# Four layers in one kernel: layer 1's taps from a queue, gate products on another engine, group norms' products in other places, the first input in thirds

## The chip, the cores and the metric

One core of a Trainium2 chip. The kernel's engines run side by side and meet at semaphores: TensorE (PE, with its weight loads PEld), VectorE (DVE), ScalarE (ACT), GpSimd (POOL) and SyncE (SP, which issues most DMAs). The metric is the device time of one execution, in microseconds. Every engine works through its own list of instructions in order; where an instruction waits, everything behind it on that engine waits too.

## What is computed

The input x is four images of 256 channels and 48 x 48 positions, in float32. Four layers follow, each `x = x + layer(group_norm(x))`:

- Layer 0: attention over the 2,304 positions with 8 heads of 64 and normed queries and keys, then a projection.
- Layer 1: a gate. The normed x goes through a 3x3 maximum and a blur with stride 3 to a 16 x 16 map; four depthwise convolutions with long, thin kernels are summed; a sigmoid of that, enlarged to 48 x 48, multiplies the normed x.
- Layer 2: one attention of width 64 over all positions, a projection, and a batch norm over the four images.
- Layer 3: a channel gate, a 3x3 depthwise convolution, an instance norm and a leaky ReLU.

```python
s = x_h1 + x_w1 + x_h2 + x_w2                  # four depthwise convolutions of the 16 x 16 map
gate = jax.nn.sigmoid(att)                     # att: s after a batch norm with given statistics
gate_up = gate[:, :, idx_h][:, :, :, idx_w]
return x[:, :c] * gate_up
...
x = x + _L1_conv_ref(_gn(x), ...)              # _gn: 32 groups of 8 channels
```

## The kernel before

Channels lie on the partitions, in two halves (k = 0, 1) of 128. Three images' x stay in SBUF; the fourth takes the first one's place when that has been sent to DRAM.

**Order.** The order of instructions on all five engines is written out by hand (`manual_schedule`): each engine's list is the order in which the Python code emits. `attend` (L393) walks over a list of *groups*. A group is two blocks of 128 keys against 384 queries of a pair of heads. Nine groups (slots 0 to 8) make a *unit*, six units a *phase* (one pair of heads of one image), four phases an image. So there are 16 phases of layer 0, 864 groups; then four phases of three units for layer 2, and after them layer 3.

For group t, `attend` emits: the score matmuls (L246) and the exponentials on ACT (L252); then the sum of the previous group's exponentials (`add_up`: L277 on POOL adds two of them into `half`, L286 and L292 on DVE add into `acc`); what is `due`; in slot 2 one early step of the layer-1 lane; the `fills` of this slot, sorted by a rank; the other lanes; and last the value matmuls (L266) of the previous group, after a unit's end also the copy of their sums on ACT (L339).

**Slot 2 (AT_AFTER % 9)** holds the chunk of the next pair's projection. By rank: 1, q's matmuls and its eviction on ACT (L528, L544); 2, v's (L559, L564); 2.5, the first half of the output projection of an earlier unit (L610 on PE, L615 on DVE, which adds the result to x); 3, k's matmuls, its eviction and two sums of squares on ACT (L550); 4, the second half of the output projection. (For image 0 the first half has rank 0.) Jobs without a rank count as 5. All of these take PSUM tiles from one pool of two, `pj`, so a matmul waits until an earlier tile has been read by ACT or DVE.

**Layer 1** of images 0 to 2 runs as a lane in the layer-0 phases of the next image (`l1_all`), that of image 3 in layer 2's phases, in another form (`l1_last`). A lane is a generator; `paced` lets it take its steps in chosen slots. Its parts: a group norm `gn`, `maxima` (DVE, L727 to L763, also ahead of the fills of slot 2), `padded`, then `strips`: 81 taps, each a product of a shifted 16 x 16 window with a per-channel weight on ACT (L789). They go in 20 rounds, five taps in the first and four in the others, two rounds ahead of the round that DVE adds up (L807), through three buffers. A round is a step, taken in slots 2, 4, 6 and 8. Then `gated`: the sigmoid by an exponential, and for three thirds of x a product with the gate (L913, on POOL for images 0 to 2, on DVE for image 3) and an addition on DVE (L915).

**`gn`** gathers statistics (L182), joins them (L187), and needs two small matmuls with `gmat` to spread them over a group's channels (L190, L200), each with some small DVE work, the second with a power on POOL (L165); the results are `rs`, `nm` and `nb`. It is a lane as well, so its matmuls stand at the end of whichever slot its steps fall into.

**Start.** `load_x(0)` brings image 0's halves, one DMA from SP and one from ACT; DVE takes statistics of 12 pieces (L179), `gn` follows, then the weights are scaled on ACT (L491), and the first projections run (L528). ACT also issues the small constants' loads (L113 to L134) and loads its function table (L154).

Of the kernel before, what the change touches and what calls it, by code (L numbers as in the profile page):

```python
# [9 lines left out]
F32 = mybir.dt.float32  # L10
# [4 lines left out]
P = 128  # L15
# [59 lines left out]
def usual_path(  # L75
# [28 lines left out]
    def load_x(b):  # L104
        for k in range(NK):
            eng = nc.scalar if b == 0 and k else nc.sync
            eng.dma_start(X[b][:, k, :], xv[:, k, b, :])

# [61 lines left out]

    def gn(b, res, halves=range(NK), slices=range(NSL), first=False):

        if "st" not in res:
            res["st"] = small.tile([P, NK, NSL, 6], F32, tag="gn_st", name="gn_st")
        st = res["st"]
        if first:
            for k in halves:
                for s in slices:
# [10 lines left out]
        ps = pj_tile()  # L189
        nc.tensor.matmul(ps[:, 0:NK], lhsT=gmat, rhs=mv[:, :, 0], start=True, stop=True)  # L190
        gm = small.tile([P, NK], F32, tag="gn_gm", name="gn_gm")
        nc.vector.tensor_copy(gm, ps[:, 0:NK])
        dev = small.tile([P, NK], F32, tag="gn_dev", name="gn_dev")
        nc.vector.tensor_sub(dev, mv[:, :, 0], gm)
        sq = small.tile([P, NK], F32, tag="gn_sq", name="gn_sq")
        nc.vector.tensor_mul(sq, dev, dev)
        nc.vector.tensor_add(sq, sq, mv[:, :, 1])
        yield 2
        ps = pj_tile()
        nc.tensor.matmul(ps[:, 0:NK], lhsT=gmat, rhs=sq, start=True, stop=True)  # L200
        gv = small.tile([P, NK], F32, tag="gn_gv", name="gn_gv")
        nc.vector.tensor_scalar(gv, ps[:, 0:NK], GN_EPS, None, ALU.add)
        rs = small.tile([P, NK], F32, tag="gn_rs", name="gn_rs", bufs=6)
        rsqrt(rs, gv)
        yield 2
        nm = small.tile([P, NK], F32, tag="gn_nm", name="gn_nm", bufs=6)
        nc.vector.tensor_scalar(nm, gm, -1.0, None, ALU.mult)
        nb = small.tile([P, NK], F32, tag="gn_nb", name="gn_nb", bufs=6)
        nc.vector.tensor_mul(nb, nm, rs)
        res["rs"], res["nb"], res["nm"] = rs, nb, nm  # L210
        yield 1
# [156 lines left out]
    due, fills, clock = {}, {}, {}  # L368

    FREE = 10**6  # L370
    AT_TOTAL, AT_FOLD, AT_INVERT, AT_DIVIDE, AT_AFTER = 3, 2, 5, 9, 11

# [20 lines left out]
    def attend(phases):  # L393
# [22 lines left out]
        def do(table, t, which=lambda rank: True):  # L416

            jobs = [job if isinstance(job, tuple) else (5, job) for job in table.pop(t, ())]
            table[t] = [job for job in jobs if not which(job[0])]
            for _, fn in sorted((job for job in jobs if which(job[0])), key=lambda job: job[0]):  # L420
                fn()

        for t, (u, g, st) in enumerate(groups):
# [18 lines left out]
            if prev is not None:  # L442
# [3 lines left out]
                if pg == NG - 1:  # L446
                    last(pu, t)
            prev = (u, g)
        pu, pg = prev
# [327 lines left out]
    def strips(b, k, norm, res):  # L777
# [6 lines left out]
        ]  # L784

        def products(n):
            for i, t in enumerate(ROUNDS[n]):
                dr, dc = TAPS[t]
                nc.scalar.activation(  # L789
                    bufs[n % 3][:, :, min(n, 1) + i].rearrange("p (r c) -> p r c", c=AS),  # L790
                    pd[:, PAD + dr : PAD + dr + AS, PAD + dc : PAD + dc + AS],
                    AF.Identity, scale=wt[:, k, t : t + 1],
                )

# [95 lines left out]
    def gated(b, k, norm, res):  # L890
# [19 lines left out]
        for i in range(4):  # L910
            if i < 3:
                eng = nc.gpsimd if b < NX else nc.vector
                eng.tensor_mul(xg[:, :, i], xg[:, :, i], up)  # L913
            if i > 0:
# [142 lines left out]
    def l1_all(b):  # L1057
# [3 lines left out]
        start = clock["t"]  # L1061
        ahead = gn(b, norm)
        for _ in range(NSL - 1):
# [10 lines left out]
        for k in range(NK):  # L1074
# [109 lines left out]
    for i, (b, p) in enumerate(order):  # L1184
# [1296 lines left out]
```

## Time and profile before

| | us |
|---|---|
| time, median of 3 runs (range) | 3,684.39 (3,683.62 to 3,686.41) |
| the profiled execution | 3,686.69 |
| its span, first to last instruction | 3,685.0 |
| first score matmul of layer 0's groups | 47.5 |
| first score matmul of layer 2's groups | 2,965.1 |

Rows of the page's costliest groups (line, engine, operation, output and inputs, count, then busy time and the mean of one in ns, then the engine's idle time before them and what ended it):

```profile
L252 ACT ACTIVATE pt<-sc 128x768 f32<-128x768 f32 x1944 | 1476.4, 812 | 790.0 <-PE sc L246 787.5
L277 POOL TENSOR_TENSOR half<-pt 128x768 f32<-128x768 f32 x477 | 939.9, 1972 | 1729.0 <-ACT pt L252 1650.1
L292 DVE TENSOR_TENSOR acc<-acc,pt 128x768 f32<-128x768 f32 x792 | 885.2, 1118 | 84.4 <-DVE acc L292 2.3
L789 ACT ACTIVATE prod<-pd,wt 128x256 f32<-128x256 f32 x486 | 280.9, 745 | 0.2
```

Durations of one instruction overlap the next one's where an engine is busy without a break, so the distance from start to start is the better price there; both are told where they differ. An idle time before a matmul with a name behind it is a wait; what is idle on another engine costs nothing by itself.

### The profile page before, as it was taken

To read this page: it belongs to the slowest core of one execution; us is meant where nothing else is said; L and a number is where in the kernel's file an instruction comes from. 1 tells how busy PE (TensorE), PEld (TensorE's weight loads), DVE (VectorE), ACT (ScalarE), POOL (GpSimd) and SP (SyncE) were. 2 spreads that over 40 slices of the span, in tenths; PEclk is the share of its full clock that TensorE was granted. 3 is DMA by queue.
4 is the path that set the end of the run, shared out by engine and by line. 5 is a ranking of instruction groups with operands and counts; after the bars stand their busy time and mean duration, and the time that the engine had idled before them with its cause. 6 is when DMAs were issued, how large, how long until landed. Compare 5 with 4: busy or idle time off the path is not lost.

```text
span 3685.0 us, 86525 instructions
## 1 busy us (share of the span) xinstructions
PE 3516.1 (95%) x36338; PEld 1766.9 (48%) x36338; DVE 2520.1 (68%) x3209; ACT 2343.6 (64%) x3814; POOL 1423.6 (39%) x899
## 2 busy tenths in 40 slices
PE   8999999999999999999999999999999999999685
PEld 4554545554444444544444445444444445654343
DVE  3455555476778676767786667667967787576687
ACT  4565666566875885568758856687587555555353
POOL 2333333333343334333433343334333456664232
PEclk9999999999999999999999999999999999999797
DMA  2111111111111111311111111111111100000001
GB/s 90 47 26 22 26 21 25 21 29 18 26 21 25 21 25 21 76 21 25 21 25 21 25 21 25 21 25 21 25 17 25 17 6 6 6 8 4 26 34 70
DMA packets 112959, 95.53 MB, mean 26 GB/s; under 512 B 56128, under 2 KB 110000, under 8 KB 110768
## 3 DMA queue, kind: packets, MB, share of 16 engines
q1 hardware_dynamic: 109952, 87.73, 13.0%
q8 instruction: 286, 4.69, 0.5%
q10 hardware_dynamic: 2608, 2.18, 0.2%
q14 instruction: 113, 0.93, 0.1%
HBM read 56.97 MB, written 11.80 MB: 19 GB/s over the span
## 4 chain that ended last, share of the span: by engine, by line
PE 71%; DVE 14%; issue 6%; ACT 5%; POOL 4%; DMA 1%; SPq 0%; DVEq 0%; ACTq 0%; POOLq 0%
PE sc L246 27%; PE av L266 27%; PE pj L528 6%; DVE acc L292 5%; PE pj L610 3%; PE pj L559 3%; POOL half L277 2%; DVE sc L1471 2%; ACT pt L252 2%; PE pj L299 1%; ACT prod L789 1%; DVE av L1471 1%; PE pj L851 1%; DVE acc L286 1%; PE pj L967 1%
## 5 line engine op out<-in xcount | busy, mean ns | idle before, releaser
L252 ACT ACTIVATE pt<-sc 128x768 f32<-128x768 f32 x1944 | 1476.4, 812 | 790.0 <-PE sc L246 787.5
L277 POOL TENSOR_TENSOR half<-pt 128x768 f32<-128x768 f32 x477 | 939.9, 1972 | 1729.0 <-ACT pt L252 1650.1
L246 PE MATMUL sc<-q,k 64*64 64x384 f32 x13824 | 1280.1, 485 | 9.8 <-ACT pt L252 9.4
L266 PE MATMUL av<-pt,v 64*64 64x384 f32 x13824 | 1280.4, 485 | 0.0
L292 DVE TENSOR_TENSOR acc<-acc,pt 128x768 f32<-128x768 f32 x792 | 885.2, 1118 | 84.4 <-DVE acc L292 2.3
L246 PEld LDWEIGHTS sc<-q,k 64*64 64x64 f32 x13824 | 510.1, 133 | 636.2 <-issue 498.7
L266 PEld LDWEIGHTS av<-pt,v 64*64 64x64 f32 x13824 | 514.7, 133 | 590.7 <-issue 554.8
L292 DVE TENSOR_TENSOR acc<-acc,half 128x768 f32<-128x768 f32 x459 | 473.6, 1032 | 349.2 <-POOL half L277 348.3
L615 DVE SCALAR_TENSOR_TENSOR x<-pj,bo,x 128x384 f32<-128x384 f32 x192 | 118.2, 616 | 512.3 <-PE pj L610 512.0
L789 ACT ACTIVATE prod<-pd,wt 128x256 f32<-128x256 f32 x486 | 280.9, 745 | 0.2
L528 PE MATMUL pj<-xs,w 128*128 128x384 f32 (+1 forms) x720 | 275.4, 505 | 0.0
L347 POOL TENSOR_TENSOR o<-o,rinv 128x384 f32<-128x384 f32 x95 | 125.9, 1326 | 238.7 <-DMA rinv<-rinv 224.5
L528 PEld LDWEIGHTS pj<-xs,w 128*128 128x128 f32 x720 | 124.1, 189 | 127.9 <-issue 38.3
L610 PE MATMUL pj<-o,wo 128*128 128x384 f32 x384 | 160.7, 503 | 22.1 <-DVE x L615 17.9
L266 PE MATMUL av<-pt,qv 64*64 64x384 f32 x1728 | 174.6, 497 | 0.0
L246 PE MATMUL sc<-qv,kd 64*64 64x384 f32 x1728 | 169.7, 486 | 2.4 <-ACT pt L252 2.4
L807 DVE TENSOR_REDUCE prod<-prod 128x256 f32<-128x1280 f32 x114 | 168.6, 1479 | 0.0
L559 PEld LDWEIGHTS pj<-w,xs 128*128 128x128 f32 x1080 | 134.5, 191 | 24.1
L286 DVE TENSOR_TENSOR acc<-pt 128x768 f32<-128x768 f32 x99 | 131.7, 1331 | 12.5 <-ACT pt L252 12.5
L559 PE MATMUL pj<-w,xs 128*128 128x128 f32 x1080 | 134.9, 275 | 0.0
L544 ACT ACTIVATE k<-pj,bias 128x384 f32<-128x384 f32 x90 | 52.2, 580 | 106.6 <-PE pj L528 106.2
L343 POOL TENSOR_TENSOR o<-raw 128x384 f32<-128x384 f32 x95 | 112.2, 1182 | 0.0
(235 smaller groups left out, 2716.6 us busy)
## 6 DMA issues: line engine op xcount, KB each, us to landing
xs<-in_x_dram SPq DMA_DIRECT2D x90, 384.0 KB
rinv<-rinv SPq DMA_DIRECT2D x208, 94.5 KB
out_dram<-x SPq DMA_DIRECT2D x6, 1152.0 KB
l<-row SPq DMA_DIRECT2D x416, 1.5 KB
w<-in_wqkv_dram SPq DMA_DIRECT2D x32, 192.0 KB
x<-in_x_dram SPq DMA_DIRECT2D x5, 1152.0 KB
rinv<-ls SPq DMA_DIRECT2D x208, 1.5 KB
x_out<-x SPq DMA_DIRECT2D x6, 384.0 KB
```

The costliest lines, as they stand in the source:

```text
L246: nc.tensor.matmul(ps[c * D : (c + 1) * D, h, :SL], lhsT=u["of"]["k"][r, j0 : j0 + D], rhs=u["of"]["q"][r, u["qc"]], start=True, stop=True,)
L252: nc.scalar.activation(pt, ps[:, :, :SL], AF.Exp, scale=u["scale"])
L266: nc.tensor.matmul(u["av"][h * D : (h + 1) * D, half, :SL], lhsT=value(u, j, h)[r], rhs=pt[r, h, :], start=j == 0, stop=j == JB - 1,)
L277: nc.gpsimd.tensor_add(half, pts[0], pts[1])
L286: nc.vector.tensor_add(u["acc"], ready[0], ready[1])
L292: nc.vector.tensor_add(u["acc"], u["acc"], term)
L347: eng.tensor_mul(o, o, u["rinv"])
L528: nc.tensor.matmul(ps[:, :n], lhsT=at["w"][:, k, t, :], rhs=xs[s][:, k, :n], start=k == 0, stop=k == NK - 1,)
L559: nc.tensor.matmul(ps[:, i * P : (i + 1) * P], lhsT=xs[s][:, k, i * P : (i + 1) * P], rhs=at["w"][:, k, 2, :], start=k == 0, stop=k == NK - 1,
L610: nc.tensor.matmul(ps[:, :SL], lhsT=wo[:, p, k * P : (k + 1) * P], rhs=o["o"], start=True, stop=True,)
L789: nc.scalar.activation(bufs[n % 3][:, :, min(n, 1) + i].rearrange("p (r c) -> p r c", c=AS), pd[:, PAD + dr : PAD + dr + AS, PAD + dc : PA ...
L807: nc.vector.tensor_reduce(to, bufs[n % 3][:, :, : min(n, 1) + len(taps)], AX.X, ALU.add)
```

## The change

- `load_x(0)` issues each half in three parts of 768 columns, half by half in turn; the statistics of image 0 are taken in the order of the columns.
- `gn` has its two matmuls and what follows them in functions, and a way to place them: with `placed=True` the first goes, as a fill of rank 3.5, into the next slot 2, the second into slot 2 of the unit after, and `nb` is worked out three slots later. It is used for both norms of `l1_all` and for the next image's layer-0 norm; `l1_all` waits for `nb` before its taps.
- `strips` puts taps into a queue, `taps_due`. After a fill of rank 1, 2, 3 or 4 one is taken; at the end of a slot as many as `QUOTA` names; before a round is added up, whatever is left of it.
- The gate's products of images 0 to 2 run on DVE.

```diff
     def load_x(b):
-        for k in range(NK):
-            eng = nc.scalar if b == 0 and k else nc.sync
-            eng.dma_start(X[b][:, k, :], xv[:, k, b, :])
+        parts = 3 if b == 0 else 1
+        for i in range(parts):
+            cols = slice(i * N // parts, (i + 1) * N // parts)
+            for k in range(NK):
+                eng = nc.scalar if b == 0 and k else nc.sync
+                eng.dma_start(X[b][:, k, cols], xv[:, k, b, cols])
...
-    def gn(b, res, halves=range(NK), slices=range(NSL), first=False):
+    def gn(b, res, halves=range(NK), slices=range(NSL), first=False, placed=False):
...
+        def squares():
+            ps = pj_tile()
+            nc.tensor.matmul(ps[:, 0:NK], lhsT=gmat, rhs=mv[:, :, 0], start=True, stop=True)
+            nc.vector.tensor_copy(gm, ps[:, 0:NK])
...
+        def inverse():
+            ps = pj_tile()
+            nc.tensor.matmul(ps[:, 0:NK], lhsT=gmat, rhs=res["sq"], start=True, stop=True)
...
+        if placed:
+            t = clock["t"] + 1
+            t += (AT_AFTER - t) % NG
+            fills.setdefault(t, []).append((3.5, squares))
+            fills.setdefault(t + NG, []).append((3.5, inverse))
+            due.setdefault(t + NG + 3, []).append(done)
+            yield 1
+            return
...
+    taps_due = []
+    QUOTA = (2, 1, 0, 1, 2, 1, 2, 1, 2)
+    def take_taps(n):
+        for _, fn in taps_due[:n]:
+            fn()
+        del taps_due[:n]
+    EVICTED = (1, 2, 3, 4)
...
-            for _, fn in sorted((job for job in jobs if which(job[0])), key=lambda job: job[0]):
+            for rank, fn in sorted((job for job in jobs if which(job[0])), key=lambda job: job[0]):
                 fn()
+                if rank in EVICTED:
+                    take_taps(1)
...
                 if pg == NG - 1:
                     last(pu, t)
+            take_taps(QUOTA[clock["slot"]])
...
         def products(n):
             for i, t in enumerate(ROUNDS[n]):
-                dr, dc = TAPS[t]
-                nc.scalar.activation(
...
+                taps_due.append((n, lambda i=i, t=t: tap(n, i, t)))
...
         for n, taps in enumerate(ROUNDS):
             last = n == len(ROUNDS) - 1
+            take_taps(sum(1 for of, _ in taps_due if of <= n))
...
-                eng = nc.gpsimd if b < NX else nc.vector
-                eng.tensor_mul(xg[:, :, i], xg[:, :, i], up)
+                nc.vector.tensor_mul(xg[:, :, i], xg[:, :, i], up)
...
-        ahead = gn(b, norm)
+        ahead = gn(b, norm, placed=True)
...
+            while "nb" not in norm:
+                yield ROUND
             yield from strips(b, k, norm, res)
...
-        yield from gn(b, norm2, [1])
+        yield from gn(b, norm2, [1], placed=True)
...
-            others.append((gn(b + 1, norms0[b + 1]), GN_TICKS, 0, n - 2))
+            others.append((gn(b + 1, norms0[b + 1], placed=True), NSL + 1, 0, n - 3 * NG))
```

More of the change, by code (lines that the diff above doesn't have):

```diff
@@ L176, in gn @@
         if first:
-            for k in halves:
-                for s in slices:
+            for s in slices:
+                for k in halves:
                     nc.vector.bn_stats(st[:, k, s, :], X[b][:, k, s * SL : (s + 1) * SL])
@@ L187, in gn @@
             nc.vector.bn_aggr(mv[:, k, :], st[:, k].rearrange("p s f -> p (s f)"))
-        yield 3
[L189 to L195, printed above, removed]
@@ L196, in gn @@
-        nc.vector.tensor_mul(sq, dev, dev)
-        nc.vector.tensor_add(sq, sq, mv[:, :, 1])
-        yield 2
[L199 to L204, printed above, removed]
-        yield 2
-        nm = small.tile([P, NK], F32, tag="gn_nm", name="gn_nm", bufs=6)
@@ L207, in gn @@
[L207 to L210, printed above, removed]
+        gm = small.tile([P, NK], F32, tag="gn_gm", name="gn_gm")
+        def squares():
+            ps = pj_tile()
+            nc.tensor.matmul(ps[:, 0:NK], lhsT=gmat, rhs=mv[:, :, 0], start=True, stop=True)
+            nc.vector.tensor_copy(gm, ps[:, 0:NK])
+            dev = small.tile([P, NK], F32, tag="gn_dev", name="gn_dev")
+            nc.vector.tensor_sub(dev, mv[:, :, 0], gm)
+            res["sq"] = sq = small.tile([P, NK], F32, tag="gn_sq", name="gn_sq")
+            nc.vector.tensor_mul(sq, dev, dev)
+            nc.vector.tensor_add(sq, sq, mv[:, :, 1])
@@ new lines, in inverse, with done @@
+        def inverse():
+            ps = pj_tile()
+            nc.tensor.matmul(ps[:, 0:NK], lhsT=gmat, rhs=res["sq"], start=True, stop=True)
+            gv = small.tile([P, NK], F32, tag="gn_gv", name="gn_gv")
+            nc.vector.tensor_scalar(gv, ps[:, 0:NK], GN_EPS, None, ALU.add)
+            res["rs_"] = small.tile([P, NK], F32, tag="gn_rs", name="gn_rs", bufs=6)
+            rsqrt(res["rs_"], gv)
+        def done():
+            rs = res["rs_"]
+            nm = small.tile([P, NK], F32, tag="gn_nm", name="gn_nm", bufs=6)
+            nc.vector.tensor_scalar(nm, gm, -1.0, None, ALU.mult)
+            nb = small.tile([P, NK], F32, tag="gn_nb", name="gn_nb", bufs=6)
+            nc.vector.tensor_mul(nb, nm, rs)
+            res["rs"], res["nb"], res["nm"] = rs, nb, nm
@@ L211, in gn @@
+        if placed:
[6 more added lines that the diff above has]
+            return
+        yield 3
+        squares()
+        yield 2
+        inverse()
+        yield 2
+        done()
         yield 1
@@ L784, in strips, with tap @@
         ]
+        def tap(n, i, t):
+            dr, dc = TAPS[t]
+            nc.scalar.activation(
+                bufs[n % 3][:, :, min(n, 1) + i].rearrange("p (r c) -> p r c", c=AS),
+                pd[:, PAD + dr : PAD + dr + AS, PAD + dc : PAD + dc + AS],
+                AF.Identity, scale=wt[:, k, t : t + 1],
+            )
         def products(n):
             for i, t in enumerate(ROUNDS[n]):
-                dr, dc = TAPS[t]
[L789 to L793, printed above, removed]
+                taps_due.append((n, lambda i=i, t=t: tap(n, i, t)))
         products(0)
```

## Prediction

> **What bounds the kernel now.** I read the page first: one execution of 3,686.69 us, span 3,685.0.
>
> ```profile
> PE 3516.1 (95%) x36338; PEld 1766.9 (48%) x36338; DVE 2520.1 (68%) x3209; ACT 2343.6 (64%) x3814; POOL 1423.6 (39%) x899
> ```
>
> TensorE is 95% busy, so only what makes it wait, or what it has to do itself, can move the end. The change touches the layer-0 phases alone (16 of them, six units of nine slots each), the work of layer 1 hung into them, and the first 47 us. Second view: busy time in windows, one window a phase, bounds read from the timeline as the start of every 54th group of score matmuls (columns: us, then PE, PEld, DVE, ACT, POOL, clock).
>
> ```profile
> 577.90:755.70 177.80, 177.75 (x1932) 89.53 (x1928) 90.96 (x123) 108.41 (x172) 59.17 (x38) 1.00 0.14 22
> 939.10:1127.70 188.60, 185.59 (x1936) 87.80 (x1932) 140.67 (x172) 138.38 (x233) 70.81 (x42) 0.98 0.14 24
> ```
>
> A phase without layer-1 work takes 177.8 us. The twelve with it run from 755.7 to 2,965.1, so 2,209.4 us, 184.1 each: 75 us more than twelve plain ones. About 13 us of that is the chunk slot's other order for images 1 to 3 (8.34 us against 8.15, and 8.97 against 8.78, in a plain unit's slot 2, 66 times); it stays. The other 62 us are what the change can reach. Third view: TensorE's waits inside 755.7:2965.1 (total, times, longest).
>
> ```profile
> PE pj L610 <- DVE x L615: 17.9, 11, 2.9
> PE sc L246 <- ACT pt L252: 9.1, 11, 1.3
> PE pj L988 <- DVE bias L942: 1.9, 1, 1.9
> ```
>
> The rest are pauses too short for this list, found by laying each unit's slot starts beside a plain unit's (2.58 us a slot, 21.28 us for the eight slots other than slot 2), and three stretches at half clock (1105.7 for 6.8 us, 1846.4 for 3.4, 2795.3 for 6.8), each right after a wait; they cost half their length, 8.5 us.
>
> **Taps one by one.** Now 486 taps (L789) stand in ACT's order in runs of four, six of them of five; in the changed order they stand in runs of one (206), two (104) or three (24). The worst case of a run, in the timeline:
>
> ```profile
> 901.65 2.83 ACT L789 ACTIVATE prod<-pd,wt 128x256 f32<-128x256 f32 x5
> 904.26 1.55 ACT L252 ACTIVATE pt<-sc 128x768 f32<-128x768 f32 x2
> 905.18 1.56 PE L246 MATMUL sc<-q,k 64*64 64x384 f32 x16 [1.32 <-ACT pt L252]
> ```
>
> Five taps push the two exponentials back, and the next scores find no free PSUM tile. Outside slot 2, a unit with four runs of four takes 21.75 to 22.08 us instead of 21.28, the first unit of a stretch 22.88, the last before a pair's end about 22.23. Summed over six stretches (5.17, 5.12, 5.18, 5.11, 5.16, 4.9): 30.6 us.
>
> What stays: a slot has 2.58 us, two exponentials take 1.40 from start to start, so one or two taps fit (0.52 each) and three overrun by 0.38. Slot 8 gets three and slot 0 two behind the copy of the value sums (0.69); I work out a lag near 1.0 us when slot 1 begins. Today's run of four makes a lag of 0.87 (exponentials 1.76 after the slot's start against 0.89) and costs 0.1 to 0.25. So I leave 0.3 us a unit for 28 units, 8.5 us: **gain 22**, between 14 (lag as costly as today in two slots) and 29.
>
> A tap between evictions hides in the gap: q's eviction starts at 3.00 in slot 2, v's at 4.33 (waiting for TensorE), k's at 6.46. After 0.48 for q there are 0.85 us for one tap of 0.52; after v there are over 1.5. No cost while ACT enters slot 2 less than 0.33 us late.
>
> Here a page speaks against the change. The Trainium skill, ScalarE: Activation LUTs, "What ACT_TABLE_LOAD costs": back-to-back ACTIVATEs overlap by about 93 ns. Break the 366 joints inside runs and, by that rule, ACT loses 34 us, over a microsecond a unit. The trace's starts say otherwise: tap to tap 519 ns, tap to exponential 516, exponential to tap 691 against 708 to another exponential. The overlap is with whatever is queued behind. I take the row: no extra ACT time.
>
> **Gate products.** Eighteen L913 leave POOL for DVE. The row has both: on POOL 2,307 ns median, on DVE (the last image) 944. What they do now, in the timeline:
>
> ```profile
> 1096.76 2.56 DVE L292 TENSOR_TENSOR acc<-acc,half 128x768 f32<-128x768 f32 x1
> 1099.43 3.84 DVE L292 TENSOR_TENSOR acc<-acc,pt 128x768 f32<-128x768 f32 x2
> 1100.14 2.31 POOL L913 TENSOR_TENSOR x<-x,gate 128x768 f32<-128x768 f32 x1
> 1103.19 0.94 DVE L286 TENSOR_TENSOR acc<-pt 128x768 f32<-128x768 f32 x1
> 1104.33 0.95 DVE L915 TENSOR_TENSOR x<-x,l1acc 128x768 f32<-128x768 f32 x1
> 1105.19 0.61 DVE L615 SCALAR_TENSOR_TENSOR x<-pj,bo,x 128x384 f32<-128x384 f32 x1
> 1105.86 1.65 PE L610 MATMUL pj<-o,wo 128*128 128x384 f32 x2 [2.92 <-DVE x L615]
> ```
>
> DVE's additions take 2.56 us and 1.9 instead of 0.96 wherever POOL works beside them; the backlog ends in L615, which holds the PSUM tile that the second half of the output projection needs. Five of the eleven L610 waits belong to gates (2.92, 0.70, 2.94, 2.77, 0.69: 10.0 us), and the half clock at 1105.7 and 1846.4 follows two of them (3.4 + 1.7). In all 15. After: each of those slots has one product more on DVE (0.94), queued before L615, but three POOL products fewer in the 15 us before it. Redoing the chain from 1088 with 0.96 an addition, plus the rest of a POOL operation where one runs beside it, the last addition ends about 1101.7, L615 at 1102.3; k's matmuls end at 1102.9. No wait, 0.6 us spare. **Gain 13** (2 left for the others), between 4 and 15. The six other L610 waits (maxima L727, L752 ahead of L615; 7.9 us) and the one at L988 with its half clock stand in the same order after: kept.
>
> **Group norms' products.** Nine norms, 18 matmuls, move from the end of a slot into slot 2, behind k's projection (rank 3.5) and ahead of the output projection's second half. Their present price reads from units that differ in nothing else: 22.23 against 21.28, 0.95 us for the two. In the new place each takes the PSUM tile that L615 frees, and the second half then gets the same tile, so it waits for the small matmul and for DVE's read of it. Nearest row, in the prologue: matmul start 15.18, DVE copy 15.78 to 15.94, then the semaphore: 0.83 us each, 1.66 for two. **Loss 6.4** (9 x 0.71), between 2 (if the first read overlaps k's eviction and switching the array's tiling is saved) and 8. The later `nb` delays nothing: taps begin in the same place of ACT's order, two units after.
>
> **First x in thirds.**
>
> ```profile
> 15.86 1.28 ACT L154 ACT_TABLE_LOAD   x1 [15.86 <-DMA Ww<-in_W_w_dram]
> 19.10 1.12 ACT L491 ACTIVATE w<-w,gn_rs 128x384 f32<-128x384 f32 x2 [1.75 <-PE pj L484]
> ```
>
> x is whole at 8.96 and twelve L179 (0.47 each) follow. In thirds only four are left after the last: the chain that ends in L484 comes 3.7 us earlier. But ACT issues eleven small loads first, and the earliest still waits for x's last piece (9.17 before), so the table load and the warm-up still end at 17.35, and L491 can begin 1.75 us earlier, not 3.7. **Gain 1.75**, between 0.5 and 2.5. SP issues two more loads (0.4 each) and its second weight load waits for the first third; all land well before L484. The Trainium skill, DMA: Bandwidth & Descriptors, "Measured": batch to 1 MiB for 75% of peak, with 138 GB/s at 64 KB. At 240 GB/s (my estimate between its rows) 2.36 MB would take 9.8 us and eat the gain. The windows 3:6 and 6:9 show 396 and 375 GB/s, but in pieces of 1.15 MB; thirds queue without a pause (issues 0.4 us apart), so I take the row.
>
> **Sum.** 22 + 13 + 1.75 - 6.4 = 30.4 us off 3,686.7: 3,656.3. The profiled run lies 2.3 us above the median of those shown, so **3,654**.
>
> **Rivals.**
> 1. The finer taps leave no lag at all (every slot but 8 and 0 has room): 30 instead of 22. 3,646. Chance 0.15.
> 2. VectorE becomes the bound at the gates: it is 75% busy there and the product sits ahead of L615. If the waits stay at 10 us and the clock falls with them, gain 13 goes: 3,667. For it: 0.6 us is a small margin; against: POOL's 2.3 us slowed three additions each time. Chance 0.12.
> 3. Forced takes: the queue lags, rounds are drained in bursts before L807. The order shows no run over three, but three in slot 8 and the copy behind it could cost as much as runs of four: 3,676. Chance 0.10.
> 4. The other side: a tap ahead of v's or k's eviction. Past 0.33 us of lag at slot 2, every further microsecond is paid by v, then k, in full, in 30 units. At 1.4 us of lag it is 1.1 x 30 = 33 us, which cancels the rest; at 1.8 it is 3,698. ACT is 85% busy in tap stretches, which speaks against a lag that lasts. Chance 0.03, and 0.03 for a sum within the noise.
>
> The forecast has 0.57. The range, 3,638 to 3,670, takes in rivals 1 and 2 and the bounds of the tap and norm terms. About 0.2% (7.4 us) is what a measurement can tell: faster 0.94, same 0.03, slower 0.03.
>
> **What would show it.** Phases with taps: 22.2 us or more outside slot 2 falling to 21.3 to 21.6, and no wait on L252 over 0.3 us. L610's waits on L615: six left, some 8 us, and no half clock near gates. The second half of L610 waiting 0.4 to 0.5 us, 18 times, behind a gmat matmul. L491 at 17.3 with the table load before it unmoved. I am wrong if v's eviction starts later in slot 2 than 4.33, or if DVE is still adding at the gates when k's matmuls end.

## The result, and the profile after

Median 3,660.6 us (3,657.7 to 3,663.2, four runs) against 3,685.4 (3,683.6 to 3,686.8, four runs) before: ratio 0.9933, 95% interval 0.9916 to 0.995, some 25 us. The profiled execution has a span of 3,658.6 us, 26.4 less than before. It divides like this (phases 0 to 3 have no layer-1 work and take 708.3 and 708.6 us):

| part of the span, us | before | after |
|---|---|---|
| first score matmul | 47.48 | 47.01 |
| twelve phases with layer-1 work | 2,209.4 | 2,183.2 |
| in these: 72 units outside slot 2, above 21.28 each | 40.7 | 12.1 |
| in these: the 72 slots 2 | 636.6 | 638.9 |
| in these, inside and outside slot 2: half clock | 8.5 | 3.4 |
| layer 2 to the end | 719.9 | 719.9 |

(Half clock costs half the length of the stretches that the trace's clock record gives for it.) The last row is equal by chance, as e3 below shows. The gain lies outside slot 2: the taps no longer stand in runs, and the norms' products (0.95 us for two) have left. In slot 2, where they went, what the gates give is used up. Of the 26.2 us of the twelve phases 5.1 are half clock. The page's first row and two phases (columns as before: window, PE, PEld, DVE, ACT, POOL, clock, DMA share, GB/s):

```profile
PE 3499.3 (96%) x36338; PEld 1778.0 (49%) x36338; DVE 2617.0 (72%) x3227; ACT 2381.9 (65%) x3814; POOL 1389.8 (38%) x881
```

```profile
577.71:755.58 177.87, 177.82 (x1932) 89.57 (x1928) 91.16 (x124) 108.32 (x172) 58.61 (x38) 1.00 0.15 24
937.18:1120.21 183.03, 181.15 (x1936) 88.69 (x1932) 161.47 (x178) 146.31 (x238) 68.22 (x39) 1.00 0.16 25
```

The plain phase is as it was; the second window is the same phase 5 that took 188.6. VectorE is busier, 161 us against 141, with only six operations more, three of them gate products: its additions are stretched more often than before (L316, once L292, takes 1,215 ns in the mean of the whole kernel, 1,118 before). TensorE's waits between 750 and 2,939 us (total, times, longest):

```profile
PE pj L648 <- DVE x L653: 6.9, 6, 1.7
PE sc L270 <- ACT pt L276: 4.9, 29, 0.2
PE pj L196 <- DVE x L653: 2.8, 3, 1.0
PE pj L1029 <- DVE bias L983: 2.5, 1, 2.5
PE pj L648 <- DVE gn_gm L197: 1.8, 7, 0.3
PE pj L648 <- DVE gn_gv L208: 1.8, 7, 0.3
```

(L648 and L653 are the output projection and its addition, L610 and L615 before; L270 and L276 scores and exponentials; L196 and L206 the norm's products.) The long waits for exponentials are gone, but 29 short ones, all alike, have come. The waits for L653 fell from 17.9 to 6.9, plus 2.8 where the norm's product now stands in front and does the waiting. These nine are the six that are not at gates (three of them now at L196) and three new ones of 0.6 to 0.7: the first units of phases 5 and 9, and the last of phase 15. The 14 waits of 0.3 for DVE's reads of the norm's products are new.

The 29 alike are one place, the first scores of slot 2 in units with taps; they need the PSUM tile that slot 1's exponentials free (timeline, ACT, then PE):

```profile
1001.75 0.80 ACT L363 COPY raw<-av 128x768 f32<-128x768 f32 x1
1002.45 1.29 ACT L826 ACTIVATE prod<-pd,wt 128x256 f32<-128x256 f32 x2
1003.53 1.55 ACT L276 ACTIVATE pt<-sc 128x768 f32<-128x768 f32 x2
1004.96 0.78 ACT L826 ACTIVATE prod<-pd,wt 128x256 f32<-128x256 f32 x1
1005.50 1.57 ACT L276 ACTIVATE pt<-sc 128x768 f32<-128x768 f32 x2
```

```profile
1004.43 1.57 PE L270 MATMUL sc<-q,k 64*64 64x384 f32 x16 [0.17 <-ACT pt L276]
```

Behind three taps in slot 8, the copy and two more taps hold the exponentials of slot 1 back by 1.1 us. The wait shows as 0.17; in the distance between starts it costs 0.35 (slot 1 takes 2.93 instead of 2.58). Below, where no profile line is shown, a wait is given by what it adds to the distance between the starts of two matmuls. What is left of the lag costs another 0.10 among slot 2's own scores.

The gate that cost 2.92 us before (unit 5 of phase 5), now:

```profile
1095.76 2.57 DVE L310 TENSOR_TENSOR acc<-pt 128x768 f32<-128x768 f32 x1
1098.25 1.75 DVE L954 TENSOR_TENSOR x<-x,gate 128x768 f32<-128x768 f32 x1
1099.93 0.95 DVE L956 TENSOR_TENSOR x<-x,l1acc 128x768 f32<-128x768 f32 x1
1100.80 0.61 DVE L653 SCALAR_TENSOR_TENSOR x<-pj,bo,x 128x384 f32<-128x384 f32 x1
```

The addition ends at 1101.4 and the second half of the projection starts at 1101.46: no wait, but nothing to spare either. DVE's operations still take 2.57 and 1.75 instead of 0.95, beside two POOL operations (`half` at 1095.08, `o` at 1097.48) that have stayed.

### The profile page after: what moved, and what is told of

Its sections match the earlier page's. It is cut to its first block, busy times and chain, and to the rows that moved or that the text cites. A ratio compares the mean times of both kernels' runs of the same rounds, so it can differ in the third digit from the quotient of the medians.

```text
span 3658.6 us, 86475 instructions
## 1 busy us (share of the span) xinstructions
PE 3499.3 (96%) x36338; PEld 1778.0 (49%) x36338; DVE 2617.0 (72%) x3227; ACT 2381.9 (65%) x3814; POOL 1389.8 (38%) x881
## 5 line engine op out<-in xcount | busy, mean ns | idle before, releaser
L276 ACT ACTIVATE pt<-sc 128x768 f32<-128x768 f32 x1944 | 1475.3, 811 | 768.2 <-PE sc L270 759.9
L270 PE MATMUL sc<-q,k 64*64 64x384 f32 x13824 | 1273.3, 483 | 5.1 <-ACT pt L276 5.1
L316 DVE TENSOR_TENSOR acc<-acc,pt 128x768 f32<-128x768 f32 x792 | 962.1, 1215 | 81.0 <-DVE acc L316 1.9
L270 PEld LDWEIGHTS sc<-q,k 64*64 64x64 f32 x13824 | 521.0, 133 | 607.9 <-issue 537.3
L316 DVE TENSOR_TENSOR acc<-acc,half 128x768 f32<-128x768 f32 x459 | 475.1, 1035 | 306.3 <-POOL half L301 305.1
L653 DVE SCALAR_TENSOR_TENSOR x<-pj,bo,x 128x384 f32<-128x384 f32 x192 | 118.3, 616 | 435.3 <-PE pj L648 434.8
L826 ACT ACTIVATE prod<-pd,wt 128x256 f32<-128x256 f32 x486 | 335.9, 761 | 0.2
L648 PE MATMUL pj<-o,wo 128*128 128x384 f32 x384 | 162.0, 506 | 14.8 <-DVE x L653 7.2
L270 PE MATMUL sc<-qv,kd 64*64 64x384 f32 x1728 | 172.3, 491 | 2.4 <-ACT pt L276 2.4
L310 DVE TENSOR_TENSOR acc<-pt 128x768 f32<-128x768 f32 x99 | 150.6, 1521 | 10.7 <-ACT pt L276 10.7
```

What stands on the lines that cost most here:

```text
L270: nc.tensor.matmul(ps[c * D : (c + 1) * D, h, :SL], lhsT=u["of"]["k"][r, j0 : j0 + D], rhs=u["of"]["q"][r, u["qc"]], start=True, stop=True,)
L276: nc.scalar.activation(pt, ps[:, :, :SL], AF.Exp, scale=u["scale"])
L310: nc.vector.tensor_add(u["acc"], ready[0], ready[1])
L316: nc.vector.tensor_add(u["acc"], u["acc"], term)
L648: nc.tensor.matmul(ps[:, :SL], lhsT=wo[:, p, k * P : (k + 1) * P], rhs=o["o"], start=True, stop=True,)
L826: nc.scalar.activation(bufs[n % 3][:, :, min(n, 1) + i].rearrange("p (r c) -> p r c", c=AS), pd[:, PAD + dr : PAD + dr + AS, PAD + dc : PA ...
```

## The experiments

Each is the changed kernel with one edit. One profiled execution each; "twelve phases" is the cleanest column, since the first score and the part behind layer 0 differ by a microsecond or two between executions with the same instructions there. It holds the half clock of the next column, which does not always follow the same waits; a difference there has to be read without it where the edit did not move those waits. The ratio is to the kernel before, measured beside it; that kernel's own median lay between 3,683.0 and 3,685.4, so medians of different rows compare to some 2 us.

| | first score | twelve phases | half clock in these | layer 2 to end | span | median (ratio, interval) |
|---|---|---|---|---|---|---|
| before | 47.48 | 2,209.4 | 8.5 | 719.9 | 3,685.0 | 3,685.4 |
| changed | 47.01 | 2,183.2 | 3.4 | 719.9 | 3,658.6 | 3,660.6 (0.9933, 0.9916 to 0.995) |
| e1 taps in rounds | 46.16 | 2,196.1 | 3.4 | 719.5 | 3,670.3 | 3,672.5 (0.9972, 0.9961 to 0.9983) |
| e2 gates on POOL | 45.78 | 2,188.5 | 5.1 | 722.6 | 3,665.5 | 3,667.0 (0.9955, 0.9938 to 0.9971) |
| e3 norms in their lane | 46.36 | 2,185.2 | 5.1 | 717.1 | 3,656.9 | 3,660.7 (0.9943, 0.9926 to 0.9959) |
| e4 x whole | 48.80 | 2,183.2 | 3.4 | 718.9 | 3,659.5 | 3,665.9 (0.9957, 0.9941 to 0.9974) |
| e5 no tap at the copy | 46.78 | 2,171.8 | 3.4 | 719.9 | 3,647.0 | 3,652.1 (0.992, 0.9903 to 0.9936) |
| e6 norms behind the projection | 46.71 | 2,177.1 | 0 | 725.8 | 3,657.8 | 3,658.1 (0.9931, 0.9914 to 0.9948) |
| e7 table first, TensorE kept busy | 43.90 | 2,186.4 | 6.8 | 719.6 | 3,658.5 | 3,659.9 (0.9941, 0.9924 to 0.9958) |
| e8 turns moved | 46.48 | 2,228.7 | 23.9 | 717.9 | 3,701.7 | 3,705.5 (1.0062, 1.0045 to 1.0079) |
| e9 gates and norms undone | 46.94 | 2,192.8 | 6.8 | 717.1 | 3,665.1 | 3,668.4 (0.9961, 0.9947 to 0.9975) |
| e10 no piece ahead | 47.35 | 2,189.1 | 3.4 | 719.3 | 3,664.3 | 3,664.7 (0.9944, 0.9928 to 0.9961) |
| e11 three mended | 43.79 | 2,168.6 | 1.7 | 716.1 | 3,636.6 | 3,641.4 (0.9889, 0.9873 to 0.9906) |

### One part undone: e1 to e4

**Taps.**

```diff
-                taps_due.append((n, lambda i=i, t=t: tap(n, i, t)))
+                tap(n, i, t)
```

> The changed kernel with one part undone: a round's four or five taps are issued together again, at the round's turn; gate products, norms' places and x in thirds stay changed. Theory (from the two traces): units with taps go back from 21.63 us outside slot 2 to 21.75 to 22.08 (first of a stretch 22.88), the twelve phases lose 17 us, span about 3,676, time about 3,677.5. Prediction's own term: 22 us, 3,682.5. Rival (the taps gain less than the traces seem to say, because VectorE's relief at the gates shortens the lag of a run of four too): under 10 us, below 3,670.

12.9 us more in the twelve phases (half clock as in the changed kernel), 11.7 of span: above the rival, below both the theory and the prediction's 22. Outside slot 2 the loss goes from 12.1 up to 32.3, as expected (20.2). But slot 2 becomes 7.2 shorter, 631.7 against 638.9. So the queue costs 7 us in slot 2. Of these 5.9 can be named: the 0.10 of lag in each tap unit (2.5); two new waits for L653 at the first unit of phases 5 and 9 (0.83 and 0.80), where VectorE's additions run late ahead of two statistics; a copy on POOL (L510) that the projection waits for (1.2); and 0.6 more at L1029 (layer 2's first projection, in phase 15).

**Gates.**

```diff
-                nc.vector.tensor_mul(xg[:, :, i], xg[:, :, i], up)
+                eng = nc.gpsimd if b < NX else nc.vector
+                eng.tensor_mul(xg[:, :, i], xg[:, :, i], up)
```

> The changed kernel with the eighteen gate products back on POOL, all else as changed. Theory: the five waits of the output projection's second half at the gates (10 us before) and the two half-clock stretches behind two of them (5 us) come back at units 5/5, 7/3, 9/5, 11/3, 13/5; two short new waits of 0.8 us at the first unit of image pairs stay. Time 3,672 to 3,676 (+11 to +15). Rival: the waits vanished because taps one by one spread the tap sums on VectorE, and not because the products left POOL: within 4 us of 3,660.6.

Between theory and rival: 6.9 us of span, 5.3 in the phases, of which the five units named make 4.6 and the rest is half clock behind other waits. At the five units the waits come back, but smaller (1.19, 0.85, 1.18, 0.86, 0.85: 4.9 us, where before it was 10.8 by the same measure), and no half clock follows one of them. The same gate as above, VectorE in this run:

```profile
1093.37 3.45 DVE L316 TENSOR_TENSOR acc<-acc,pt 128x768 f32<-128x768 f32 x2
1096.74 1.75 DVE L310 TENSOR_TENSOR acc<-pt 128x768 f32<-128x768 f32 x1
1098.42 2.35 DVE L957 TENSOR_TENSOR x<-x,l1acc 128x768 f32<-128x768 f32 x1
1100.69 0.60 DVE L653 SCALAR_TENSOR_TENSOR x<-pj,bo,x 128x384 f32<-128x384 f32 x1
```

```profile
1101.35 0.91 PE L648 MATMUL pj<-o,wo 128*128 128x384 f32 x2 [1.02 <-DVE x L653]
```

POOL's product runs from 1097.64 and stretches the gate's addition to 2.35, just as the prediction said. The backlog that it meets is smaller than before, though: the additions ahead take 1.75, 3.45 and 1.75 here, against 2.56, 3.84 and 0.94 before, and the first of them starts 2.4 us ahead of slot 2, where before it started 0.25 behind its beginning.

**Norms.**

```diff
-        ahead = gn(b, norm, placed=True)
+        ahead = gn(b, norm)
...
-        yield from gn(b, norm2, [1], placed=True)
+        yield from gn(b, norm2, [1])
...
-            others.append((gn(b + 1, norms0[b + 1], placed=True), NSL + 1, 0, n - 3 * NG))
+            others.append((gn(b + 1, norms0[b + 1]), GN_TICKS, 0, n - 2))
```

> The changed kernel with the norms' products back at the end of a slot, as before. Theory (a unit with a placed product takes 8.78 instead of 8.15 in slot 2, two per norm, against 0.95 for both in the old place): 0.31 us a norm, 9 norms, so 2.8 us faster than the changed kernel, 3,657.8; units with the norms at 22.2 outside slot 2 and 8.15 or 8.34 in it. Prediction's term: 6.4 faster, 3,654. Rival: the placed products keep something else from going wrong (lateness of nb ahead of taps, VectorE's waits ahead of L653), and the undone kernel is no faster or slower: 3,660 to 3,666.

The times can't tell it from the changed kernel: its span is 1.7 us shorter, with 2.1 more in the twelve phases and 2.8 less behind them. The price of a placed norm by itself is what the theory says, seen clean in image 0's one norm (phase 1, with no layer-1 work): outside slot 2 its unit goes from 22.23 to 21.28, while two slots 2 go from 8.15 to 8.78, so the phase from 178.82 to 179.14, 0.32 us longer. In the eight others it would be 2.5 us; laid unit beside unit it is 1.7, since in three of them (from phase/unit 7/5, 11/5 and 15/5 on) the price is next to nothing. Against it the lane brings gate waits back at 5/5 and 9/5 (1.52 and 1.46; the units are 2.6 longer together). The next image's norm has its second product there, and its power holds POOL for 1.41 us from 1082.52 on (at 5/5), so that VectorE waits 2.37 us for `half`; `nm` and `nb` follow on DVE among the gate's operations. Another 0.9 us is half clock behind other waits.

Behind layer 0 the one norm whose second product falls on the passage to layer 2 (image 2's second) costs more than the others. From layer 2's first score to a product behind layer 2 (L1586, L1543 before) the changed kernel takes 470.5 us, this run 467.7, e9 467.9 and the kernel before 467.8: 2.7 us for that one place. (The other runs with the placed norm have 468.7 to 473.5; e11, without it, has 466.2.) The table's equal 719.9 hides it, for behind L1586 before has 252.1 us and the changed kernel 249.4, with a stretch of half clock 3.4 us longer and a wait 1.1 us longer; no part of the change lies there.

**x.**

```diff
-        parts = 3 if b == 0 else 1
+        parts = 1
```

> The changed kernel with the first x loaded in two whole halves. Theory: the first score matmul starts at 47.5 us instead of 47.0, so 0.5 us slower, 3,661.1; the weight scaling at 19.1 instead of 17.75, but half clock until 23.7 instead of 24.1. Prediction's term: 1.75 slower, 3,662.4. Both below what the times can tell: read in the trace.

The weight scaling at 19.34 and the first score at 48.80: 1.8 later than in the changed kernel's profile, and not 0.5. The difference from my reading is one of chance, and the other runs show it. ACT and the first matmuls of the changed kernel:

```profile
16.35 1.28 ACT L158 ACT_TABLE_LOAD   x1 [16.35 <-DMA w<-in_attn_w_dram]
17.75 1.10 ACT L529 ACTIVATE w<-w,gn_rs 128x384 f32<-128x384 f32 x2
```

```profile
15.81 1.01 PE L522 MATMUL pj<-gn_nb,w 128*128 128x1 f32 x4 [1.24 <-DVE gn_nb L217]
18.40 2.93 PE L566 MATMUL pj<-x,w 128*128 128x384 f32 x4 [1.58 <-ACT w L529]
```

Four matmuls in 2.93 us, 0.64 from start to start, are half speed (later ones take 0.32). From the first projection to the first entry of the clock record, at full speed, it took 5.71 us here, 3.05 in e2, 3.45 in e1, 6.08 in e4, 3.91 before, with the same instructions. Over nine executions with thirds the first score lies at 45.8 to 47.4, mean 46.6; the two with whole x at 47.5 and 48.8, mean 48.1. The thirds bring 1.5 us, give or take about one.

### Mending: e5 to e8

> The changed kernel with another share-out of the queue: after slots 0 to 8 it issues 0,1,0,2,2,2,2,2,2 taps instead of 2,1,0,1,2,1,2,1,2 (so the slot that has the raw copy of the value sums gets none, and slot 8 two instead of three). Theory: the 0.35 us wait for an exponential at slot 1, in 30 units, and the 0.10 us behind it in slot 2 come from those two slots alone (three taps, then copy and two more); both vanish, 21.28 us outside slot 2, 12 to 13 us off: 3,648. Rival: one or two taps in every slot always leave some lag (0.1 us or more a unit in each of slots 4 to 8, or the row copies with two taps in slot 3 overrun): gain under 6, 3,655 or more.

```diff
-    QUOTA = (2, 1, 0, 1, 2, 1, 2, 1, 2)
+    QUOTA = (0, 1, 0, 2, 2, 2, 2, 2, 2)
```

As the theory says: 11.6 us of span, with as much half clock as the changed kernel. Outside slot 2 the loss is 1.8 us (12.1), in slot 2 the 0.10 is gone, and L270 no longer stands in the list of waits. Two taps fit into each of slots 4 to 8, and into slot 3 behind its row copies. The same place in the timeline, ACT:

```profile
1000.62 0.80 ACT L363 COPY raw<-av 128x768 f32<-128x768 f32 x1 [0.36 <-PE av L290]
1001.31 1.52 ACT L276 ACTIVATE pt<-sc 128x768 f32<-128x768 f32 x2
```

> The changed kernel with the norms' products in the same slot, but behind the output projection's second half instead of ahead of it. Theory: of the 0.63 us that a placed product costs, 0.39 is the second half's wait for VectorE's read of the PSUM tile, and only 0.24 the product itself; behind the second half nobody waits for that read: 0.39 x 18 = 7 us off, 3,653.6. Rival: the product then waits itself for a PSUM tile (the second half's VectorE addition holds one, the first half's the other), and TensorE stands as long: 3,658 to 3,661.

```diff
-            fills.setdefault(t, []).append((3.5, squares))
-            fills.setdefault(t + NG, []).append((3.5, inverse))
+            fills.setdefault(t, []).append((4.5, squares))
+            fills.setdefault(t + NG, []).append((4.5, inverse))
```

Half of the theory holds. The 14 waits are gone, but a clean placed product still costs 0.41 us instead of 0.63 (phase 1: slot 2 at 8.56, against 8.78 in the changed kernel and 8.15 without), so 0.22 are saved and not 0.39. The rival's mechanism is there, with another reader: the product waits for the tile of k's projection, which ACT has to read first. The changed kernel, then this run, at unit 5/3:

```profile
1040.87 0.28 PE L196 MATMUL pj<-gn_mv,gmat 128*128 128x2 f32 x2
1041.39 0.91 PE L648 MATMUL pj<-o,wo 128*128 128x384 f32 x2 [0.25 <-DVE gn_gm L197]
```

```profile
1039.31 0.81 PE L648 MATMUL pj<-o,wo 128*128 128x384 f32 x2
1040.14 0.38 PE L196 MATMUL pj<-gn_mv,gmat 128*128 128x2 f32 x2
```

Of the 6.0 us that the twelve phases lost, the norms' units make 3.0. The other 3.0 lie at 6/1 and 15/0, where no norm's product stands, and are half clock: the wait at 6/1 is as long in both (1.75 and 1.79), but only in the changed kernel does half clock follow it. The stretch behind it, in the changed kernel and here (window, PE, PEld, DVE, ACT, POOL, clock, DMA share, GB/s):

```profile
1164.20:1167.60 3.40, 3.40 (x22) 1.54 (x26) 3.29 (x6) 0.00 (x0) 0.00 (x0) 0.50 0.00 0
1161.40:1164.80 3.40, 3.40 (x38) 1.94 (x41) 2.65 (x5) 0.18 (x1) 0.00 (x0) 1.00 0.19 71
```

The time is that of the rival all the same, for behind layer 0 the run is 5.9 us longer. 3.0 of them lie in layer 2: at the passage the second half of the last projection waits 2.6 us for VectorE (the changed kernel has 1.3 there), and a wait for ACT behind it is 3.4 instead of 2.1. That the last norm's new place does this was not tried by itself; e11 leaves it out. The other 3.0 lie behind L1586, where the kernel before has the same 252 us.

> The changed kernel with two things in the first 20 us: the exponential that loads ScalarE's table stands ahead of its eleven small loads, and TensorE runs extra products of x's first third (8, then one behind each of the two norm products and one behind the bias product; their results are not used). Theory: the thirds' 1.35 us at the weight scaling shrank to 0.5 because TensorE works at half clock until it has been busy for some 5 us in a row, and the earlier start only made it idle longer ahead of that (1.58 us); with the products the first projection runs at full clock from the start (0.64 us a matmul instead of 1.28), 2.8 us, and the table takes 0.9 more: first score at 43.3 instead of 47.0. Rival: full clock comes at a fixed time after the launch (24 us), busy or not: first score at 46.1 at the earliest.

```diff
+    warm = cpool.tile([P, 1], F32, name="warm")
+    nc.scalar.activation(warm, mhalf[:, 0:1], AF.Exp)
     vec = cpool.tile([P, 9, NK], F32, name="vec")
...
-    warm = cpool.tile([P, 1], F32, name="warm")
-    nc.scalar.activation(warm, mhalf[:, 0:1], AF.Exp)
...
+        def spin(n):
+            ps = pj_tile()
+            for _ in range(n if first else 0):
+                nc.tensor.matmul(
+                    ps[:, :SL], lhsT=gmat, rhs=X[b][:, 0, 0:SL], start=True, stop=True
+                )
...
         if first:
+            spin(8)
             for s in slices:
...
         squares()
+        if first:
+            spin(1)
         yield 2
         inverse()
+        if first:
+            spin(1)
...
     projs[0]["norms"]()
+    ps = pj_tile()
+    for _ in range(1):
+        nc.tensor.matmul(ps[:, :SL], lhsT=gmat, rhs=X[0][:, 0, 0:SL], start=True, stop=True)
```

The first score comes at 43.90, 2.7 before the mean of the others: the theory's mechanism, and the rival's 46.1 is out. TensorE in this run:

```profile
5.36 8.18 PE L183 MATMUL pj<-x,gmat 128*128 128x384 f32 x16 [5.36 <-DMA x<-in_x_dram]
18.09 1.56 PE L578 MATMUL pj<-x,w 128*128 128x384 f32 x4 [0.61 <-DMA rfw<-in_refine_w_dram]
```

The first projection's four matmuls take 1.56 us instead of 2.93. The time shows nothing of it: the phases are 3.3 us longer in the profiled execution, which has 3.4 us more half clock in them. One stretch of it follows a new wait of 2.06 us for POOL's copy (L510 in the changed kernel) at phase 9; why the wait is new stays open.

> The changed kernel with layer 1's pieces other than taps (maxima, blur, gate) taking turns in slots 3,4,5,6,7,8 instead of 2,2,3,5,6,8, so that none stands on VectorE ahead of the output projection's additions in slot 2. Theory: the six waits of TensorE on these additions (units 4/3, 6/1, 8/3, 10/1, 12/3, 14/1; 8.9 us together) and the half clock behind the one at 1,161 us (1.7) go: 10 off, 3,650. Rival: the pieces land on VectorE's sums in other slots and exponentials wait for free tiles instead, or the chain of pieces runs late and is pushed together at the end of a pair: no gain or a loss.

```diff
-    TURNS, ROUND, ROUND_TURNS = (2, 2, 3, 5, 6, 8), -1, (2, 4, 6, 8)
+    TURNS, ROUND, ROUND_TURNS = (3, 4, 5, 6, 7, 8), -1, (2, 4, 6, 8)
```

A miss, and not the test it was meant to be: the step that `attend` allows ahead of the fills of slot 2 is not in `TURNS` and stayed; only the pieces behind them moved. Other pieces then stood ahead of L653, statistics (L1128) at 1,073 us and the end of the blur (L795 to L797) at 1,140. Slot 2 is 40.8 us longer in all, with waits for L653 of up to 4.6 us; of the 45.5 us that the phases lose, 20.5 are half clock, nearly all of it behind these waits.

### Together: e9 to e11

> The changed kernel with two parts undone at once: gate products on POOL, norms' products at the end of a slot; taps one by one and x in thirds stay. Theory: the gate waits before (10 us and 5 us of half clock behind them) are one backlog on VectorE to which both parts added: POOL's products stretch the additions, and the norm's second product with its power on POOL lies in the same two slots (alone each brought back 4.9 and 3.0 us of wait and no half clock). Both undone, units 5/5 and 9/5 wait 2.5 us or more each, half clock follows at least one of them, and the twelve layer-1 phases are longer by more than the two single undos together (5.3 + 2.1 us): 10 us or more, span 3,668 to 3,672. Rival: the two add up or overlap: 5 to 7.4 us, span about 3,664, no half clock near gates.

The edits of e2 and e3 at once. Units 5/5 and 9/5 wait 3.12 and 3.13 us, and half clock follows the second; the phases are 9.6 longer, where the single undos give 5.3 + 2.1. Half clock behind waits that are not at gates falls differently in the three, so the five gate units are the cleaner measure: 10.2 us longer here, 4.6 in e2, 2.6 in e3. The waits and the shared backlog are as the theory has them; its span was some 3 us too high, since the part behind layer 0 took 717.1 us. VectorE and TensorE at 5/5:

```profile
1096.94 3.84 DVE L316 TENSOR_TENSOR acc<-acc,pt 128x768 f32<-128x768 f32 x2
1100.70 0.95 DVE L310 TENSOR_TENSOR acc<-pt 128x768 f32<-128x768 f32 x1
1101.57 0.15 DVE L215 TENSOR_SCALAR gn_nm<-gn_gm 128x2 f32<-128x2 f32 x1
1101.76 0.16 DVE L217 TENSOR_TENSOR gn_nb<-gn_nm,gn_rs 128x2 f32<-128x2 f32 x1
1101.84 0.95 DVE L957 TENSOR_TENSOR x<-x,l1acc 128x768 f32<-128x768 f32 x1
1102.70 0.61 DVE L653 SCALAR_TENSOR_TENSOR x<-pj,bo,x 128x384 f32<-128x384 f32 x1
```

```profile
1103.37 0.91 PE L648 MATMUL pj<-o,wo 128*128 128x384 f32 x2 [2.96 <-DVE x L653]
```

It is the picture of before at this unit, line for line. At 11/3 it is not: 0.87 us of wait here, 2.94 before. What still differs from before in these phases is the taps alone (the thirds leave them as they were: e4, 2,183.2). So the taps are worth 16.6 us there (2,209.4 against 2,192.8), and 12.9 once gates and norms are changed.

> The changed kernel in which no piece of layer 1 may go ahead of the projections in slot 2 (the last experiment with the turns moved only the pieces that follow them, the early one in slot 2 stayed). All pieces of slot 2 then stand behind the output projection on VectorE. Theory: the waits of TensorE on VectorE's output additions at units 4/3, 6/1, 8/3, 10/1, 12/3, 14/1 (8.9 us) and the half clock after the one at 1,161 us (1.7) go: span 3,648 to 3,650. Rival: each stretch of pieces needs a turn more, so gates and tap sums move to other slots, and other pieces or a tap sum meet the additions: 3,655 or more.

```diff
-                most = 1 if turns == TURNS else 0
+                most = 0
```

The rival is right. The six waits (8.9 us) become seven of 1.0 to 1.4, two units in a row at one place of each image (9.3 us in all), and the copy L510 is waited for up to 2.06. The work ahead of L653 was not a matter of one step: taken from one unit it waits in the next.

> The changed kernel with what helped in single runs: taps 0,1,0,2,2,2,2,2,2 behind the slots (-11.6 us of span), norms' products behind the output projection's second half in layer 0 (-6.0 in the twelve phases; the last image's second norm goes back to the end of a slot, since its late place cost 6 us at the passage to layer 2), table load first and TensorE kept busy in the first 18 us (-2.6 at the first score). Theory: the three touch different waits and add up: span 3,636 to 3,641, time about 3,641. Rival: VectorE's queue shifts against TensorE's slots with each of them and the waits at gates or maxima come back: 3,645 or more.

The edits of e5 and e7, and e6 for all norms but image 2's second (which goes back to its lane): 22.0 us of span below the changed kernel, as the theory has it, and 3,641.4 us; its interval lies wholly below the changed kernel's. The parts are not quite the theory's. The first score comes 3.2 earlier, and the twelve phases lose 14.6 us instead of the 17.6 that e5 and e6 showed, for 3.0 of e6's were half clock. Layer 2 is 4.3 shorter instead (466.2 against 470.5); the lane for its norm brought 2.7 in e3. This version beats both.

## Why the prediction was right, and where its steps were wrong

3,654 was forecast, 3,638 to 3,670 as the range; 3,660.6 was measured. The range held, with the right sign, and the forecast was some 7 us too low, a quarter of the gain. That the sum came nearer than its terms is luck: singly undone, taps and gates are worth 9 and 8 us less than forecast, and the norms some 6 more. The sum of 30.4 us, term by term:

| term | forecast | measured |
|---|---|---|
| taps | 22 | 12.9 (e1, phases); 16.6 with gates and norms undone (before against e9) |
| gates | 13 | 5.3 alone (e2); 9.6 with the norms (e9) |
| norms | -6.4 | +2.1 in the phases (e3), 0.9 of it half clock; -2.7 in layer 2 |
| thirds | 1.75 | 1.5 (means of nine and two executions) |

- **Taps: right in mechanism, wrong in two sizes.** The lag was placed rightly, in slot 8's three taps and in slot 0's copy with two. "0.3 us a unit for 28 units, 8.5" measured 0.35 in 30 units and some beginnings (11 outside slot 2), and 0.10 a unit besides in slot 2 (2.5). The failed step is "No cost while ACT enters slot 2 less than 0.33 us late", which looks at evictions only. At 5/2 ACT starts slot 2's exponentials 0.12 us later in the slot than in e5, and 0.10 is lost among slot 2's scores, ahead of q's matmuls: q's eviction starts at 3.10 instead of 3.00 and v's at 4.43 instead of 4.33, which was named as a sign of error. The tap between the two is not the cause: e5 has it too, with v's eviction at 4.33. And with the queue VectorE's and POOL's work meets the projection in other ways (two waits of 0.8, one of 1.2). e5 shows that the lag was the quota's and not the queue's. The row-against-rule choice stood: tap starts cost nothing extra, or e5 could not have come down to 1.8 us. The page's sentence did not speak against the change in the first place: a tap between exponentials is still back to back with them.
- **Gates: right in the result, wrong in its cause.** All five waits and both stretches of half clock are gone, 15.4 us in the five units, and the six others stayed as they were (8.9 us, before and after). The step that failed gives them to POOL's products alone. e2 returns 4.6 us of the 15.4, e3 2.6, e9 10.2, with half clock once; the last 5.2 stand only in before, where the taps too are undone. The backlog before was a sum of contributions, and the 2.9 us waits with half clock needed them together. "0.6 us spare" was none: the second half starts 0.05 us after the addition ends.
- **Norms: sizes off in both directions.** "0.83 each" measured 0.63, and less in three norms, so that the nine lose 2.0 in layer 0 and not 6.4; the last of them loses 2.7 more in layer 2, where the prediction looked for nothing. That the place also takes the power and `nb` out of the gate's way was not seen; it was worth 2.6 us.
- **Thirds: the size right by luck.** "The table load and the warm-up still end at 17.35" is wrong: half of the added loads are ACT's own, and the warm-up ends at 17.8. L529 starts at 17.75, not 17.3. What the sum left out is TensorE's half speed, which ends at a different time in each execution: the profile of the changed kernel shows a gain of 0.5, the mean of the executions 1.5. The choice against the page's fall of rate with size stood: in thirds the windows 3:6 and 6:9 show 405 and 387 GB/s, before 396 and 375.
- **The sum.** Undone singly, the taps, gates and norms are worth 12.9 + 5.3 + 2.1 = 20.3 us of the 26.2 that the twelve phases gained, and 16.9 without the 1.7 us of half clock by which e2 and e3 each exceed the changed kernel. The other 6 to 9 belong to no part alone; the gate units hold most of them. Of the rivals, the first (no lag at all) is refuted by the 29 waits, the third (the lag costs as much as runs of four) is refuted by e1, the second (VectorE becomes the bound at gates) by the empty list at gates, the fourth by a lag of 0.12 at slot 2 instead of more than 0.33.

## What to carry to other kernels

Where one wait is fed by a queue of several small jobs, do not give the whole wait to the job that is to be moved: price the backlog job by job, for undoing any one here brought back less than its share, and undoing two more than their sum. When work is cut fine to fill gaps, add up what else stands in each gap (here the copy of the value sums), and give a gap only what it holds; that share-out was worth as much as the cutting. A small matmul between large ones that share two PSUM tiles cost more than its own time on either side: 0.63 us ahead of the second half, which waited for its reader, and 0.41 behind it, where it waited itself for an earlier one. And read a single profile's difference of 2 or 3 us only after the half clock in both has been laid side by side.

## What the runs showed of the hardware that was not expected

The half speed at TensorE's start ended 3.05 to 6.08 us after the first projection's start, in eleven executions with the same matmuls there. Where TensorE had been kept busy from 5.4 us on (e7; 5.3 in e11), it had ended by 11.0 and 9.5 us, ahead of the first projection. The clock column says 1.00 in that stretch, since the trace's clock record begins with the first change; only the distance of the matmuls tells it. In layer 0 each stretch of half clock was 3.41 us long or twice that. The three maxima waits of 1.4 to 1.9 us stood in each kernel but e8 and e10, and in seven of these eleven profiles half clock followed one of the three, not always the same one (at 1,164 us in the changed kernel, 1,893 in e3, 2,623 in e2), in four of them none. A wait of 3.12 us in e9 had none behind it, one of 3.13 had. The Trainium skill, TensorE: Matmul & The Clock Gate, "What's actually happening", puts this down to a free-running window of some 3.4 us in which the activity is counted; that fits the chance in these numbers, while its "±500ns" for the start is narrower than the 3 us seen here.
